# Sums of exponentials of an attention: folded on VectorE and summed by one small product, instead of a full product, a copy and a trip by DRAM

## The chip, the core and the metric

The kernel runs on one core of a Trainium2 chip. The metric is the device time of one execution in microseconds. Before the change it is 2647.13 us, the median of three runs (2646.86 to 2647.53). The profile is that of one execution, whose span is 2649.3 us. The engines are called TensorE (PE in the profile, its weight loads PEld), VectorE (DVE), ScalarE (ACT) and GpSimd (POOL); SyncE issues most of the loads.

## The reference, cut to what matters

Two graph layers over 16 graphs of 1024 nodes with 256 channels, all in float32. The first layer ends in an attention with four heads of 64 channels each:

```python
g = relu(einsum('bcn,bnm->bcm', fea, Wg) * para)      # queries, from the graph
kv = x @ kv_w                                          # keys and values
attn = softmax(einsum('bhnd,bhmd->bhnm', q, k) * scale, axis=-1)
out = einsum('bhnm,bhmd->bhnd', attn, v)
x = x + out
```

The second layer aggregates over the graph, then has two linear maps with batch normalisation. The change touches only the denominator of the softmax: for each query and each head the sum of the exponentials over 1024 keys.

## The kernel before, in words

**Units.** The attention is cut into 64 units: 16 graphs (b), 2 pairs of heads (k) and 2 halves of the queries (f, 512 each). A unit has two heads, numbered e. Scores are made transposed, keys on the partitions and queries along the columns. A unit is done in four steps (NG = 4), each over two blocks of 128 keys, so there are 256 steps and 16 of them to a graph.

**A step.** `attention()` writes the program step by step, and each engine runs its own instructions in that order; nothing reorders them later. In step s come: the scores of step s (`scores`, line 859 on TensorE, and the exponentials, line 867 on ScalarE); what is due at the top of the step; the additions of this step's exponentials into `acc` (lines 886 and 889 on VectorE); the values product of the step before (line 900); and then pieces of background work until a share of the graph's background is done. The background is everything else of the neighbouring graphs: keys and values, queries, the aggregation of the second layer, its first linear map, the norms. Its pieces have products on TensorE (line 159) and, behind them, evacuations and element-wise work on VectorE and ScalarE. A background piece may ask to be placed at the top of a step (`TOP`), as the transposes of line 384 do. `soon` puts an action behind the next piece.

**A unit's end.** When the values of a unit's last step are written, in step s = 4 x (number + 1), `acc` holds, for each of 128 partitions, two rows of 512 partial sums, one for each head. What is missing is the sum over the partitions. `sums()` makes it on TensorE at once: a product with 64 columns of ones for each head (line 917), so that every output row holds the sums. ScalarE copies the result into a tile `row` (line 919), GpSimd sends one row of each head to DRAM (line 920) and loads it back with the queries on the partitions (line 925). `finish()`, at the top of step s+2 (s+3 in graph 0, s+1 for the last two units), turns the unit's output with four transposes (line 935), and `add_output()` takes the reciprocal (line 943), multiplies (944), adds to x (950) and notes the extremes (952, 953).

**Buffers.** `ps_t` is one bank of PSUM, shared by the sums and the turned output. `row` is one of the four buffers of the tag `y`, which also serve the hidden layer's output (line 712), the columns of line 188, and `graph()`, which prepares combinations of the adjacency matrix on GpSimd during graph 0 and writes them to DRAM (lines 265 to 274). Background products alternate between two banks (`ps_mm`). GpSimd, like the others, runs its instructions in order, DMA issues among them.

Of the kernel before, what the change touches and what calls it, by code (L numbers as in the profile page):

```python
# [10 lines left out]
F32 = mybir.dt.float32  # L11
AF = mybir.ActivationFunctionType
ALU = mybir.AluOpType
AX = mybir.AxisListType
# [3 lines left out]
P = 128  # L18
# [5 lines left out]
def gnn_two_layers_kernel(  # L24
# [12 lines left out]
    nc = tc.nc  # L37
    B, N, C = x.shape
    H1 = w1_t.shape[1]
    NT = N // P  # L40
    CC = C // P
    HC = H1 // P
    HD = C // HEADS
    FB = 512
    NH = N // FB
# [6 lines left out]
    const = ctx.enter_context(tc.tile_pool(name="const", bufs=1))  # L52
    dram = ctx.enter_context(tc.tile_pool(name="dram", bufs=1, space=DRAM))

    ident = const.tile([P, P], F32, name="ident")
# [14 lines left out]
    y1_d = [dram.tile([P, HC, FB], F32, name=f"y1_d{i}") for i in range(B * NH)]  # L70

    dinv_d = dram.tile([N], F32, name="dinv_d")
    sums_d = [dram.tile([2, FB], F32, name=f"sums_d{u}") for u in range(B * CC * NH)]

    UNITS = B * CC * NH
    seen = const.tile([P, 2, UNITS], F32, name="seen")
    ones = const.tile([P, HD], F32, name="ones")
    nc.gpsimd.memset(ones, 1.0)

    def rsqrt(dst, src, add, tmp):  # L80

        nc.gpsimd.tensor_scalar_add(tmp, src, add)
        nc.gpsimd.tensor_tensor(dst, tmp, neg_half[:, : dst.shape[1]], op=ALU.pow)  # L83

    def layers(shifted):
# [9 lines left out]
        p1 = st.enter_context(tc.tile_pool(name=f"p1_{kind}", bufs=1))  # L95
        p2 = st.enter_context(tc.tile_pool(name=f"p2_{kind}", bufs=2))
        p3 = st.enter_context(tc.tile_pool(name=f"p3_{kind}", bufs=3))
        p8 = st.enter_context(tc.tile_pool(name=f"p8_{kind}", bufs=8))
        py = st.enter_context(tc.tile_pool(name=f"py_{kind}", bufs=4))
# [6 lines left out]
        ps_t = st.enter_context(tc.tile_pool(name=f"ps_t_{kind}", bufs=1, space=PSUM))  # L106
# [13 lines left out]
        def advance(pieces):  # L120

            due = queue[:]
            queue.clear()
            cost = next(pieces, None)
            for action in due:
                action()
            return cost

        def run(*parts):
            for part in parts:  # L130
                while advance(part) is not None:
                    pass
            while queue:
                queue.pop(0)()
# [75 lines left out]
        row, diag, col, deg, tmp_deg, dinv = (deg_sm[:, i, :] for i in range(6))  # L210
# [75 lines left out]
        class Norm:  # L286
# [3 lines left out]
            def __init__(self, b, first):  # L290
                tag = "a" if first else "b"
                self.src = xs[b]
                self.st6 = p2.tile([P, NT, 6], F32, tag="st6", name=f"st6_{tag}_{b}")
                self.mv = p2.tile([P, NT, 2], F32, tag="mv", name=f"mv_{tag}_{b}")
                self.sm = p2.tile([P, 3, NT], F32, tag="lnsm", name=f"lnsm_{tag}_{b}")
                self.csum = None
                if first:
                    self.csum = p2.tile([P, NT], F32, tag="csum", name=f"csum_{b}")
                    csums[b] = self.csum
                self.h = p2.tile([P, NT, C], F32, tag="h", name=f"h_{tag}_{b}")  # L300
                hs[tag, b] = self.h
# [569 lines left out]
        class Unit:  # L871
# [19 lines left out]
            def values(self, g, prs):  # L891
# [15 lines left out]
                if g == NG - 1:  # L907
                    self.os = p2.tile([P, FB], F32, tag="os", name=f"os_{self.name}")
                    nc.scalar.copy(self.os, self.o)

            def sums(self):

                u = self.index
                pt = ps_t.tile([P, FB], F32, tag="t", name=f"sums_{self.name}")
                for e in range(2):
                    r = slice(e * HD, (e + 1) * HD)
                    nc.tensor.matmul(pt[r, :], ones, self.acc[:, e, :], start=True, stop=True)
                row = py.tile([P, FB], F32, tag="y", name=f"row_{self.name}")
                nc.scalar.copy(row, pt)  # L919
                nc.gpsimd.dma_start(  # L920
                    out=sums_d[u], in_=row.rearrange("(e r) c -> e r c", r=HD)[:, 0, :]
                )
                self.inv = p2.tile([P, FB // P, 2], F32, tag="inv", name=f"inv_{self.name}")
                for e in range(2):
                    nc.gpsimd.dma_start(  # L925
                        out=self.inv[:, :, e], in_=sums_d[u][e].rearrange("(j q) -> q j", q=P)
                    )

            def finish(self):
# [10 lines left out]
            def add_output(self):  # L940
                b, k, f = self.at
                J, pt = FB // P, self.out
                nc.vector.reciprocal(self.inv, self.inv)
                nc.vector.tensor_mul(
                    self.os.rearrange("p (j e c) -> p j e c", j=J, e=2),
                    pt.rearrange("p (j e c) -> p j e c", j=J, e=2),
                    self.inv.unsqueeze(3).to_broadcast([P, J, 2, HD]),
                )
                dst = xs[b][:, f * J : (f + 1) * J, k * P : (k + 1) * P]
                nc.vector.tensor_add(dst, self.os.rearrange("p (j c) -> p j c", c=P), dst)  # L950
                inv = self.inv.rearrange("p j e -> p (j e)")
                nc.vector.tensor_reduce(seen[:, 0, self.index : self.index + 1], inv, AX.X, ALU.max)
                nc.vector.tensor_reduce(seen[:, 1, self.index : self.index + 1], inv, AX.X, ALU.min)
                if k == CC - 1:
                    complete.add((b, f))

        def attention():

            units = [Unit(b, k, f) for b in range(B) for k in range(CC) for f in range(NH)]
            steps = [(u, g) for u in units for g in range(NG)]  # L960
            per_graph = CC * NH * NG
            before = None
            pending = []
            bg, done, total, top = iter(()), 0.0, 0.0, False
            for s in range(len(steps) + 2):
                if s < len(steps):
                    unit, g = steps[s]
                    b = unit.at[0]
                    if s % per_graph == 0:
                        run(bg)  # L970
                        top = False
                        bg, done = background(b), 0.0
                        total = (37.6 if b > 0 else 41.0) * (b + 1 < B) + 24.0 * (b > 0) + 6.0 * (b + 2 < B)
                        total += 13.7 * (0 < b < B - 2) + 27.4 * (b == B - 1) + 3.0 * (b == 0)

                        total -= 10.3 * (b == B - 1)
                    made = scores(*unit.at, g)
                    due = total * (s % per_graph + 1) / per_graph
                else:
                    due += 5.1  # L980
                ended = None
                if pending and pending[0][1] <= s:
                    ended = pending.pop(0)[0]
                    ended.finish()
                if top:
                    done += advance(bg)
                    top = False
                if ended is not None:
                    ended.add_output()
                if s < len(steps):  # L990
                    for pr in made:
                        unit.add(pr)
                if before is not None:
                    (last, g_last), prs = before
                    last.values(g_last, prs)
                    if g_last == NG - 1:
                        last.sums()


                        later_by = 3 if last.at[0] == 0 else 2  # L1000
                        pending.append((last, s + (later_by if last.index < UNITS - 2 else 1)))
                while done < due and not top:
                    cost = advance(bg)
                    if cost is None:
                        break
                    if cost == TOP:
                        top = True
                        break
                    done += cost
                before = (steps[s], made) if s < len(steps) else None  # L1010
            run(bg)

        with st:
# [22 lines left out]
            else:  # L1036
# [20 lines left out]
                load_x(2)  # L1057
                run(weave(plain_queries(0), (0, weighers[0]), (5, Norm(1, True).all())))
                attention()
                attn.close()  # L1060
                turns.append(second(kind))
# [267 lines left out]
    ext = fp.tile([P, 4], F32, name="ext")  # L1329
# [8 lines left out]

    def flag(good):

        nc.tensor.matmul(good[0:1, :], ext[:, 2:3], ones[:, 0:1], start=True, stop=True)
        nc.vector.tensor_scalar(bad, good[0:1, :], -1.0, float(P), op0=ALU.mult, op1=ALU.add)

    with tc.manual_schedule():
        layers(False)

    again = nc.values_load(bad[0:1, 0:1], min_val=0, max_val=P)  # L1347
    with tc.If(again > 0):
        layers(True)
# [37 lines left out]
```

## Time and profile before

| | busy us | share of 2649.3 us |
|---|---|---|
| TensorE | 2571.1 | 97% |
| VectorE | 1741.8 | 66% |
| ScalarE | 1335.5 | 50% |
| GpSimd | 561.2 | 21% |

| lines of the sums | engine | count | mean ns |
|---|---|---|---|
| 917 product with ones | TensorE | 256 passes | 592, overlapping |
| 919 copy to `row` | ScalarE | 64 | 586 |
| 920 row to DRAM | GpSimd | 64 | 586 to issue, 1.7 us to land |
| 925 back from DRAM | GpSimd | 128 | 771 to issue, 2.7 us to land |
| 943 reciprocal | VectorE | 64 | 193 |
| 935 transposes of the output | TensorE | 256 | 286, overlapping |

A busy time adds up what an engine's instructions last. TensorE's matmuls overlap one another, so the cost of one is read from the distance between starts, not from its length. A line of the profile's timeline has the start, the length, the engine, the line of the kernel, the operation, the tiles (output <- inputs), shapes and count; in brackets stands how long the engine was idle before it and what released it. A float32 product appears as two passes, and a product of two 64-column halves as four. The clock row shows the share of TensorE's full clock that was granted. Attention begins with the scores of step 0 at 61.7 us and ends near 2324 us; then come the rest of the last graph's aggregation and the second linear map.

### The profile page before, as it was taken

The page shows a single profiled execution, that of the slowest core. Times are in us where ns is not written, and L with a number is a line of the kernel's source. Part 1 is how long each engine was busy: PE and PEld are TensorE (multiplying, and loading weights), DVE is VectorE, ACT ScalarE, POOL GpSimd, SP SyncE. Part 2 cuts the span into 40 slices and gives each one's busy share as a digit, 9 for nine tenths or more (in the row PEclk, how much of TensorE's full clock was granted, in tenths as well). Part 3 has the DMA queues.
Part 4 walks back from the last instruction along what each step waited for, and adds up shares of the span by engine and source line. Part 5 has one row for each costly group of instructions (what it writes and reads, how often), then busy time and mean ns, then how long its engine had stood idle before and what let it go on. Part 6 is the DMA issues. An engine that isn't in the chain of part 4 may idle for free. (4 is left out here: it accounts for less than half of the span.)

```text
span 2649.3 us, 32166 instructions
## 1 busy us (share of the span) xinstructions
PE 2571.1 (97%) x11874; PEld 951.7 (36%) x11874; DVE 1741.8 (66%) x2766; ACT 1335.5 (50%) x1935; POOL 561.2 (21%) x648
## 2 busy tenths in 40 slices
PE   8979999999999999999999999999999999999994
PEld 3333333333333333333333333333333333334443
DVE  5648576766667675757666676757576675557675
ACT  5745454636364554546363645545463634335544
POOL 1451111021111111110211111111111112026653
PEclk9989999999999999999999999999999999999997
DMA  4453414242423323152525242332424232355559
GB/s 159 149 177 109 146 61 171 84 171 80 166 78 135 100 96 136 60 175 80 172 80 175 68 144 92 103 133 65 166 80 171 80 132 96 134 196 204 193 179 377
DMA packets 132870, 356.12 MB, mean 134 GB/s; under 512 B 19040, under 2 KB 35936, under 8 KB 126560
## 3 DMA queue, kind: packets, MB, share of 16 engines
q1 hardware_dynamic: 105952, 274.77, 29.7%
q0 software_dynamic: 26752, 79.20, 8.9%
q8 instruction: 96, 1.57, 0.2%
q14 instruction: 70, 0.57, 0.1%
HBM read 279.19 MB, written 74.72 MB: 134 GB/s over the span
## 5 line engine op out<-in xcount | busy, mean ns | idle before, releaser
L867 ACT ACTIVATE p<-sc 128x1024 f32<-128x1024 f32 x512 | 495.4, 1020 | 610.3 <-PE sc L859 609.8
L889 DVE TENSOR_TENSOR acc<-acc,p 128x1024 f32<-128x1024 f32 x384 | 470.9, 1226 | 135.5 <-ACT p L867 115.1
L859 PE MATMUL sc<-q,k 64*128 64x512 f32 x2048 | 510.2, 617 | 14.2 <-ACT p L867 14.2
L900 PE MATMUL o<-p,v 128*64 128x512 f32 x2048 | 497.6, 607 | 0.0
L159 PE MATMUL pg<-w,h_a 128*64 128x512 f32 x1600 | 358.1, 592 | 3.4 <-ACT k L600 1.7
L159 PE MATMUL pa<-aht,h_b 128*64 128x512 f32 x1536 | 343.7, 592 | 0.0
L859 PEld LDWEIGHTS sc<-q,k 64*128 64x128 f32 x2048 | 176.6, 186 | 335.0 <-issue 298.0
L920 POOL DMA_DIRECT2D sums_d<-row x64 | 37.5, 586 | 1031.8 <-ACT row L919 1031.8
L159 PE MATMUL py<-at,w 128*64 128x512 f32 x1024 | 230.4, 592 | 0.0
L900 PEld LDWEIGHTS o<-p,v 128*64 128x64 f32 x2048 | 124.6, 136 | 286.0 <-issue 284.5
L413 DVE SCALAR_TENSOR_TENSOR w<-w,adj 128x1024 f32<-128x1024 f32 x128 | 158.0, 1235 | 101.7 <-ACT w L434 97.8
L159 PEld LDWEIGHTS pg<-w,h_a 128*64 128x64 f32 x1600 | 115.5, 137 | 231.8 <-issue 213.1
L159 PEld LDWEIGHTS pa<-aht,h_b 128*64 128x64 f32 x1536 | 111.2, 137 | 212.6 <-issue 196.6
L713 ACT ACTIVATE y<-py,vec 128x512 f32<-128x512 f32 x128 | 87.6, 684 | 167.9 <-PE py L159 111.4
L426 ACT ACTIVATE w<-cbc,csum 128x512 f32<-128x512 f32 x256 | 170.0, 715 | 0.0
L886 DVE TENSOR_TENSOR acc<-p,p 128x1024 f32<-128x1024 f32 x64 | 78.9, 1233 | 109.3 <-ACT p L867 109.3
L714 POOL DMA_DIRECT2D y_d<-y x128 | 70.1, 547 | 316.1 <-ACT y L713 315.5
L434 ACT ACTIVATE w<-w 128x1024 f32<-128x1024 f32 x128 | 134.9, 1054 | 1.8
L488 DVE TENSOR_TENSOR w<-w,w 128x1024 f32<-128x1024 f32 x112 | 132.7, 1215 | 1.5
L925 POOL DMA_DIRECT2D inv<-sums_d x128 | 98.2, 771 | 138.7 <-DMA sums_d<-row 102.2
L159 PEld LDWEIGHTS py<-at,w 128*64 128x64 f32 x1024 | 74.3, 137 | 145.1 <-issue 128.2
L717 DVE BATCH_NORM_STATS2 stats<-y 128x6 f32<-128x512 f32 x128 | 85.4, 686 | 59.3 <-ACT y L713 57.4
(151 smaller groups left out, 2892.9 us busy)
## 6 DMA issues: line engine op xcount, KB each, us to landing
aht<-aht_d SPq DMA_DIRECT2D x224, 512.0 KB, 6.4
adj<-in_adj_dram SPq DMA_DIRECT2D x128, 512.0 KB, 4.4
y_d<-y POOLq DMA_DIRECT2D x128, 256.0 KB, 2.6
yin_f<-y_d SPq DMA_DIRECT2D x32, 1024.0 KB, 6.3
x<-in_x_dram SPq DMA_DIRECT2D x32, 512.0 KB, 5.0
para<-in_para_dram SPq DMA_DIRECT2D x64, 256.0 KB, 3.8
x_d<-x POOLq DMA_DIRECT2D x16, 1024.0 KB, 10.5
xo_f<-x_d SPq DMA_DIRECT2D x32, 512.0 KB, 8.7
```

The lines of the kernel that those rows point to most:

```text
L159: nc.tensor.matmul(dst[r], left[:, r], right, start=start, stop=stop)
L413: nc.vector.scalar_tensor_tensor(w, w, 1.0, a, op0=ALU.add, op1=ALU.mult)
L426: nc.scalar.activation(w[:, t, :], cbc[:, q * FB : (q + 1) * FB], AF.Abs, bias=csum[:, th * TH + t : th * TH + t + 1], scale=-1.0,)
L434: nc.scalar.activation(made[i], made[i], AF.Tanh, scale=-0.5 / C)
L488: nc.vector.tensor_sub(block(i)[part], block(x)[part], block(y)[part])
L713: nc.scalar.activation(y, made, AF.Identity, bias=b1[:, j : j + 1])
L717: nc.vector.bn_stats(stats1[:, j, i, :], y)
L859: nc.tensor.matmul(sc[:, e, :], ks[b][k][r, m * P : (m + 1) * P], qs[b][k][r, f * FB : (f + 1) * FB], start=True, stop=True,)
L867: nc.scalar.activation(pr, sc, AF.Exp)
L889: nc.vector.tensor_add(self.acc, self.acc, pr)
L900: nc.tensor.matmul(self.o[r, :], vs[b][k][:, m, r], pr[:, e, :], start=(m == 0), stop=(m == NT - 1),)
L925: nc.gpsimd.dma_start(out=self.inv[:, :, e], in_=sums_d[u][e].rearrange("(j q) -> q j", q=P))
```

## The change

The sums are made in another way, with no copy by ScalarE and no trip by DRAM. At a unit's end VectorE turns `acc` of one head in squares of 32x32 into PSUM and sums each run of 32 elements (`fold`). After that, partition 32a + r holds, in column c, the sum of query 32c + r over the 32 keys of group a. What is still to be added are the four groups a. A product with the constant table `same` (ones where the row and the column have the same remainder by 32) does this for both heads at once, with only 32 columns; its output has the queries on the partitions already, and four reciprocals, one for each quarter of the partitions, put them in place in `inv`.

The steps are laid out anew: the fold of head 0 comes at the end of step s, behind that step's background, that of head 1 at the end of step s+1; the product and the reciprocals at the top of step s+2; the transposes and the addition at the top of step s+3. The last unit does all of it in s and s+1. `st6` and `mv` of the norms go from two buffers to one, and `ones` to one column.

```diff
-    sums_d = [dram.tile([2, FB], F32, name=f"sums_d{u}") for u in range(B * CC * NH)]
...
+    SQ = 32
+    NS = P // SQ
+    same = const.tile([P, NS, SQ], F32, name="same")
+    nc.vector.tensor_reduce(
+        same[:, 0, :], ident.rearrange("p (a r) -> p r a", r=SQ), AX.X, ALU.add
+    )
+    for i in range(1, NS):
+        nc.vector.tensor_copy(same[:, i, :], same[:, 0, :])
...
-                self.st6 = p2.tile([P, NT, 6], F32, tag="st6", name=f"st6_{tag}_{b}")
-                self.mv = p2.tile([P, NT, 2], F32, tag="mv", name=f"mv_{tag}_{b}")
+                self.st6 = p1.tile([P, NT, 6], F32, tag="st6", name=f"st6_{tag}_{b}")
+                self.mv = p1.tile([P, NT, 2], F32, tag="mv", name=f"mv_{tag}_{b}")
...
+            def fold(self, e):
+                if e == 0:
+                    self.part = p1.tile([P, 2, FB // SQ], F32, tag="part", name=f"part_{self.name}")
+                pt = ps_t.tile([P, FB], F32, tag="t", name=f"turned_{self.name}_{e}")
+                nc.vector.transpose(pt, self.acc[:, e, :])
+                nc.vector.tensor_reduce(
+                    self.part[:, e, :], pt.rearrange("p (c s) -> p c s", s=SQ), AX.X, ALU.add
+                )
+
             def sums(self):
-                pt = ps_t.tile([P, FB], F32, tag="t", name=f"sums_{self.name}")
-                for e in range(2):
-                    r = slice(e * HD, (e + 1) * HD)
-                    nc.tensor.matmul(pt[r, :], ones, self.acc[:, e, :], start=True, stop=True)
-                row = py.tile([P, FB], F32, tag="y", name=f"row_{self.name}")
-                nc.scalar.copy(row, pt)
-                nc.gpsimd.dma_start(
-                    out=sums_d[u], in_=row.rearrange("(e r) c -> e r c", r=HD)[:, 0, :]
-                )
+                pt = ps_t.tile([P, FB], F32, tag="t", name=f"sums_{self.name}")[:, : 2 * FB // SQ]
+                nc.tensor.matmul(
+                    pt,
+                    same.rearrange("p a r -> p (a r)"),
+                    self.part.rearrange("p e c -> p (e c)"),
+                    start=True,
+                    stop=True,
+                )
                 self.inv = p2.tile([P, FB // P, 2], F32, tag="inv", name=f"inv_{self.name}")
-                for e in range(2):
-                    nc.gpsimd.dma_start(
-                        out=self.inv[:, :, e], in_=sums_d[u][e].rearrange("(j q) -> q j", q=P)
+                for a in range(NS):
+                    r = slice(a * SQ, (a + 1) * SQ)
+                    nc.vector.reciprocal(
+                        self.inv[r].rearrange("p j e -> p e j"),
+                        pt[r].rearrange("p (e j a) -> p a e j", e=2, a=NS)[:, a],
                     )
...
-                nc.vector.reciprocal(self.inv, self.inv)
...
+                for action in at_top.pop(s, ()):
+                    action()
                 if top:
                     done += advance(bg)
                     top = False
-                if ended is not None:
-                    ended.add_output()
+                if s in adds:
+                    adds.pop(s)()
...
                     if g_last == NG - 1:
-                        last.sums()
-                        later_by = 3 if last.at[0] == 0 else 2
-                        pending.append((last, s + (later_by if last.index < UNITS - 2 else 1)))
+                        n = 0 if last.index == UNITS - 1 else 1
+                        for e in range(2):
+                            at_end.setdefault(s + n * e, []).append(lambda u=last, e=e: u.fold(e))
+                        at_top.setdefault(s + 1 + n, []).append(last.sums)
+                        at_top.setdefault(s + 1 + 2 * n, []).append(last.finish)
+                        adds[s + 1 + 2 * n] = last.add_output
...
+                for action in at_end.pop(s, ()):
+                    action()
```

More of the change, by code (lines that the diff above doesn't have):

```diff
@@ L72, in gnn_two_layers_kernel @@
     dinv_d = dram.tile([N], F32, name="dinv_d")
-    sums_d = [dram.tile([2, FB], F32, name=f"sums_d{u}") for u in range(B * CC * NH)]
     UNITS = B * CC * NH
     seen = const.tile([P, 2, UNITS], F32, name="seen")
-    ones = const.tile([P, HD], F32, name="ones")
+    ones = const.tile([P, 1], F32, name="ones")
     nc.gpsimd.memset(ones, 1.0)
+    SQ = 32
[6 more added lines that the diff above has]
+        nc.vector.tensor_copy(same[:, i, :], same[:, 0, :])
     def rsqrt(dst, src, add, tmp):
@@ L909, in values @@
                     nc.scalar.copy(self.os, self.o)
-            def sums(self):
-                u = self.index
-                pt = ps_t.tile([P, FB], F32, tag="t", name=f"sums_{self.name}")
-                for e in range(2):
-                    r = slice(e * HD, (e + 1) * HD)
-                    nc.tensor.matmul(pt[r, :], ones, self.acc[:, e, :], start=True, stop=True)
-                row = py.tile([P, FB], F32, tag="y", name=f"row_{self.name}")
-                nc.scalar.copy(row, pt)
-                nc.gpsimd.dma_start(
-                    out=sums_d[u], in_=row.rearrange("(e r) c -> e r c", r=HD)[:, 0, :]
+            def fold(self, e):
[6 more added lines that the diff above has]
+                )
+            def sums(self):
+                pt = ps_t.tile([P, FB], F32, tag="t", name=f"sums_{self.name}")[:, : 2 * FB // SQ]
[5 more added lines that the diff above has]
+                    stop=True,
                 )
                 self.inv = p2.tile([P, FB // P, 2], F32, tag="inv", name=f"inv_{self.name}")
-                for e in range(2):
-                    nc.gpsimd.dma_start(
-                        out=self.inv[:, :, e], in_=sums_d[u][e].rearrange("(j q) -> q j", q=P)
+                for a in range(NS):
[3 more added lines that the diff above has]
+                        pt[r].rearrange("p (e j a) -> p a e j", e=2, a=NS)[:, a],
                     )
@@ L962, in attention @@
             before = None
-            pending = []
+            at_top, at_end, adds = {}, {}, {}
             bg, done, total, top = iter(()), 0.0, 0.0, False
@@ L980, in attention @@
                     due += 5.1
[L981 to L984, printed above, removed]
+                for action in at_top.pop(s, ()):
+                    action()
                 if top:
@@ L1339, in flag @@
     def flag(good):
-        nc.tensor.matmul(good[0:1, :], ext[:, 2:3], ones[:, 0:1], start=True, stop=True)
+        nc.tensor.matmul(good[0:1, :], ext[:, 2:3], ones, start=True, stop=True)
         nc.vector.tensor_scalar(bad, good[0:1, :], -1.0, float(P), op0=ALU.mult, op1=ALU.add)
```

## The prediction, made before the changed kernel was run

> **What bounds the kernel now.** I read the engine totals first, then what TensorE waits for, then the stretch in which one unit of attention ends, then the place in VectorE's queue where the change puts its work.
>
> ```profile
> PE 2571.1 (97%) x11874; PEld 951.7 (36%) x11874; DVE 1741.8 (66%) x2766; ACT 1335.5 (50%) x1935; POOL 561.2 (21%) x648
> ```
> ```profile
> PE sc L859 <- ACT p L867: 14.2, 2, 13.7
> PE htp L384 <- ACT h_a L329: 8.2, 1, 8.2
> ```
> TensorE is busy 97% of the span, and the longest sum of waits of any of its lines is 14.2 us, nearly all one wait of 13.7 us. In the attention stage, then, a TensorE instruction removed shortens the run, and a wait put into TensorE's queue lengthens it by all of its length: there is almost no slack to take it from.
>
> ```profile
> 1215.66 1.94 PE L900 MATMUL o<-p,v 128*64 128x512 f32 x8
> 1217.42 1.03 PE L917 MATMUL sums<-acc,ones 128*64 128x512 f32 x4
> 1218.28 0.60 PE L159 MATMUL pk<-ht,kvw_f 128*64 128x512 f32 x2
> ```
> This is the timeline at a unit's end. The sums' product stands from 1217.42 to the next start at 1218.28: **0.86 us** of TensorE (the matmul's printed time overlaps the next one).
>
> ```profile
> 1269.65 1.99 PE L859 MATMUL sc<-q,k 64*128 64x512 f32 x8
> 1271.57 0.66 PE L935 MATMUL ot<-ident,os 128*128 128x128 f32 x4
> 1271.31 0.69 DVE L522 TENSOR_TENSOR q<-pg,q 128x512 f32<-128x512 f32 x1
> 1272.33 0.16 DVE L315 TENSOR_TENSOR lnsm_b<-lnsm_b,deg 128x4 f32<-128x4 f32 x1 [0.33 <-POOL lnsm_b L83]
> 1272.52 0.16 DVE L318 SCALAR_TENSOR_TENSOR lnsm_b<-mv_b,lnsm_b 128x4 f32<-128x4 f32 x1
> 1272.61 0.20 DVE L943 RECIPROCAL inv<-inv 128x8 f32<-128x8 f32 x1
> ```
> Two engines at one place of the program: the top of the second step after a unit's last. TensorE gets there at 1271.57, when its scores are issued (today it starts the ot transposes). VectorE has by then not finished the background of the step before: L318 ends at 1272.68, and only then comes L943, the first instruction of the top. VectorE is 1.11 us behind. Nobody minds today, since TensorE waits for nothing of VectorE here.
>
> ```profile
> 154.76 0.59 ACT L909 COPY os<-o 128x512 f32<-128x512 f32 x1 [0.73 <-PE o L900]
> 174.97 0.59 ACT L919 COPY row<-sums 128x512 f32<-128x512 f32 x1 [19.63 <-DMA aht_d<-two]
> 131.98 0.57 POOL L920 DMA_DIRECT2D sums_d<-row  x1
> 139.47 1.55 POOL L925 DMA_DIRECT2D inv<-sums_d  x2 [6.92 <-DMA sums_d<-row]
> ```
> The one long wait comes from the old way of the sums. In graph 0 the copy into row needs one of the four y buffers; they hold what graph() writes out, so ScalarE stands 19.63 us, and the exponentials behind it. The writes are late because GpSimd itself stood from 131.98 to 141.02 (9.0 us) on the trip by DRAM.
>
> ```profile
> 163.00:176.50 13.50, 0.00 (x0) 0.00 (x0) 0.76 (x1) 1.53 (x3) 13.19 (x20) 0.60 0.60 212
> 176.50:180.00 3.50, 3.46 (x9) 1.31 (x10) 0.00 (x0) 1.92 (x2) 3.34 (x6) 0.58 0.51 172
> 184.00:188.00 4.00, 4.00 (x13) 1.21 (x13) 3.69 (x4) 3.41 (x6) 0.52 (x1) 0.50 0.13 1
> 1213.00:1358.00 145.00, 144.81 (x696) 51.75 (x694) 97.99 (x157) 74.12 (x109) 22.43 (x29) 1.00 0.34 117
> ```
> Windows: length, busy PE, PEld, DVE, ACT, POOL, granted clock, DMA. The stop drops the clock to about half until some 190 us. An inner graph lasts 145 us, TensorE busy 144.8, VectorE 98: VectorE has room on the average, so what counts is where its work is put.
>
> **What the Trainium skill says.** TensorE: Matmul & The Clock Gate, Step-by-step: only weight loads are pulled ahead, matmuls stay in program order; this trace agrees, as no product passes a waiting one at 176.5. So a waiting sums product holds everything behind it. PSUM — Partial Sum Buffer, Engine vs sequencer instructions: VectorE's queue is strictly first in, first out; the trace agrees (L943 above sits behind L315's wait). The clock gate page, Part 1, names windows of about 3.4 us after which an idle array is slowed; the trace agrees in kind (clock 0.58 and 0.50 above). As a price: VectorE: DVE Perf Modes, The three transpose paths, gives 311 ns for 128x128 in 32x32 blocks, in bf16 and into SBUF; no run here shows that operation.
>
> **The change, part by part.**
>
> *TensorE.* Gone: 64 x 0.86 = 55.0 us. New: one product with 128x128 weights and 32 columns. In f32 a product is two passes; four passes of 128x128 weights and 128 columns (ot) take 0.66 us, so two take at most about 0.33, and the two passes of the one-column product L1341 take 0.16. I take 0.30, 64 x 0.30 = 19.2. Net gain **36 us**.
>
> *VectorE's fold.* A turn of 128x512 into PSUM and a sum over 32s. Price of the turn: from below 0.53 us (512 elements at one per 0.96 GHz cycle by the page's clock, no fixed cost), from above double the copy L387 (128x512 out of PSUM, 0.686 us), 1.37, if 4-byte elements go at half rate. From the page's 311 ns for 128 and this trace's slope for reduces, (1209 - 286) / 896 = 1.03 ns an element (L416, L223), I take 0.70. Sum: 286 + 384 x 1.03 = 0.68 us. With two gaps of 0.03, a fold is **1.44 us**; ends 1.2 and 2.1. Two per unit are 184 us of VectorE; four reciprocals at L943's 0.19 instead of one add 37. Off the path, on the average: 14 us more in a graph of 145 us with 47 idle.
>
> *The wait.* The second fold is queued at the end of step s+1, behind that step's background; the sums product follows the scores of step s+2 and reads it. So TensorE waits (VectorE's lag at this place) + 1.44 + 0.1 for handing over. The lag, end of the background minus start of ot (or htp), in the four units of an inner graph: 1234.42 - 1234.39 = 0.03 (behind L413); 1.11 (above); 1308.98 - 1309.21 = -0.23 (behind L307); 1344.68 - 1343.98 = 0.70 (behind L717). Sum 1.61. In the second unit the first fold, too, pushes: it falls into a stretch where VectorE is dense, with 1.0 us of gaps to swallow 1.44, so 0.4 more. Per graph 1.61 + 0.4 + 4 x 1.54 = **8.2 us**, and the same rows repeat in graphs 1 to 13: 107 us. Behind the waiting product stand the values of step s+1 and the background products; ScalarE then waits for TensorE. In the last two graphs VectorE is less loaded: by the same reading 0 to 3.8 us a unit, 14 in all, and 3 for the last unit, where no scores lie between and the transposes wait for the reciprocals too: 17. Graph 0: 4.
>
> *ScalarE and GpSimd.* 64 copies of 0.586 and 192 DMA issues go: 37 and 136 us, all off the path except in graph 0. There ScalarE needs no y buffer, and GpSimd's graph() runs at least 9 us ahead, so the column copies that use y next on VectorE hardly wait. Gained: 13.7, the 2.9 us wait after it, and half of the 9 us at half clock: **21 us**.
>
> *Later finish.* The output is added at s+3 instead of s+2 (s+3 in graph 0 already). Inner graphs start the next norm later than that anyway; for the last graph I put 3 us into the 17. Single buffers for st6 and mv: nothing, since a norm's readers are through before the next norm begins. The table same: under 1 us before x has arrived.
>
> *Clock.* Waits of 3 us come near the 3.4 us windows; if a quarter of the 13 drop it and cost about 3 us each: 10 us.
>
> Sum: 107 + 17 + 4 - 36 - 21 + 10 = +81, so 2647 + 81 = **2728 us**.
>
> **Rivals.**
> (a) *The folds are hidden*, VectorE reaching them 1.5 us earlier than I read: only the gains stay, 2647 - 36 - 21 = 2590. For it: VectorE's 66%. Against: the lag rows above, where even the best unit has only 0.23 us in hand. Chance 0.10.
> (b) *Half the waits*: a fold nearer 1.2 us and some lag gone, since TensorE itself now arrives later after each wait: 2647 - 57 + 64 = 2654, and from there to 2680. For it: VectorE catches up during a wait. Against: the lags arise within the step before, from TensorE's own products. 0.08: 0.05 of it slower, 0.02 no change, 0.01 faster.
> (c) *Turn at half rate, or clock drops at each long wait*: a fold of 2.0 adds 0.56 x 62 = 35 us, drops add 30 more: 2765 to 2800. For it: a 4-byte turn and PSUM as its target are unseen. 0.12.
>
> **How the numbers follow.** The forecast has 0.70; 2680 to 2775 holds it, the dear end of (b) and the cheap end of (c). Slower: 0.70 + 0.12 + 0.05 = 0.87; within 0.2%: 0.02; faster: 0.10 + 0.01 = 0.11.
>
> **What would show it.** Right: TensorE's waits list the sums product behind VectorE's reduce, some 62 times, about 2 us each and 110 to 140 us in all, the second unit of a graph the worst at 3; a turn and a reduce of 0.7 us each; VectorE near 1960 us busy; no 13.7 us wait in graph 0, and TensorE's busy share near 93%. Wrong: if a fold takes 1.2 us or less, or if VectorE stands ready before TensorE arrives; or if other TensorE products come to wait for VectorE's later evacuations, which I put at nothing because two banks leave each of them a product's time.

## The result, and the profile after

The changed kernel takes **2754.49 us**, the median of four runs (2751.68 to 2757.04); the kernel before took 2647.33 (2646.86 to 2648.39) beside it. The ratio is **1.0405 [1.039, 1.0421]**: 107 us slower, where 81 were forecast. The profiled run of the changed kernel has a span of 2755.1 us, against 2649.3. The profiled execution of the kernel before took 2651.18 us, 4 us more than its median, so that differences between profiles and between medians differ by some microseconds. The lines of the kernel have moved: scores are L867, values L908, the turn L925, the reduce L926, the sums product L933, the reciprocals L943, the output's transposes L954, background products L167.

First the engine totals of the changed kernel.

```profile
PE 2572.7 (93%) x11746; PEld 963.4 (35%) x11746; DVE 1957.3 (71%) x3218; ACT 1298.8 (47%) x1871; POOL 394.1 (14%) x456
```

TensorE has 128 instructions less, but not less busy time: 64 x 0.86 us were meant to leave. Part of its work now ran at a lower clock, as shown below; in e3, an experiment below with the same TensorE instructions and no such drops in the inner graphs, it is busy 2537.5 us. Its share fell from 97% to 93%: 182 us of the span are idle (2755.1 - 2572.7), against 78 before (2649.3 - 2571.1).

Next, from the waits of the changed kernel, the longest one of TensorE.

```profile
PE sums L933 <- DVE part L926: 121.8, 60, 6.3
```

Microseconds in all, times, the longest: 60 of the 64 sums products wait for VectorE's reduce, 121.8 us together. The second on TensorE's list is the wait for ScalarE's `h_a` before attention begins, 8.4 us, which was 8.2 before; the wait of 13.7 us in graph 0 is gone. Now the groups of the changed kernel that make up the new way (busy, mean ns of one, then the idle time just before).

```profile
L933 PE MATMUL sums<-part,same 128*128 128x32 f32 x128 | 27.3, 297 | 121.8 <-DVE part L926 121.8
L925 DVE STREAM_TRANSPOSE turned<-acc 128x512 f32<-128x512 f32 x128 | 91.1, 712 | 0.0
L926 DVE TENSOR_REDUCE part<-turned 128x16 f32<-128x512 f32 x128 | 88.5, 692 | 4.4
```

The turn and the reduce cost 0.71 and 0.69 us, and VectorE idles almost nowhere ahead of them: a fold starts as soon as its turn in the queue comes. That is the clue that the fold waits behind other work, not for data.

The timeline of the changed kernel at the end of the second unit of graph 1 shows one such wait.

```profile
241.89 1.99 PE L867 MATMUL sc<-q,k 64*128 64x512 f32 x8
246.98 0.41 PE L933 MATMUL sums<-part,same 128*128 128x32 f32 x2 [3.10 <-DVE part L926]
247.32 1.94 PE L908 MATMUL o<-p,v 128*64 128x512 f32 x8
...
245.40 0.16 DVE L326 SCALAR_TENSOR_TENSOR lnsm_b<-mv_b,lnsm_b 128x4 f32<-128x4 f32 x1
245.48 0.72 DVE L925 STREAM_TRANSPOSE turned<-acc 128x512 f32<-128x512 f32 x1
246.24 0.69 DVE L926 TENSOR_REDUCE part<-turned 128x16 f32<-128x512 f32 x1
```

TensorE's scores end at 243.9, and the sums product is next in its queue. VectorE gets through the background of the step before at 245.5 (L326, as foreseen), then folds until 246.93, and 0.05 later the product starts. TensorE has stood for 3.10 us. ("Second" counts the places of a graph's stretch at which a unit ends. The first place belongs to the last unit of the graph before, so the second is that of the graph's own first unit.) The other units of an inner graph wait 1.09, 1.99 and 1.38 us by the same reading; together **7.56 us** a graph. From the product's start to that of the values (246.98 to 247.32) it costs 0.34 us.

Some waits cost more than their length. Four windows of the changed kernel, two places in graph 2: length, busy PE, PEld, DVE, ACT, POOL, granted clock, DMA share, GB/s.

```profile
394.00:399.00 5.00, 1.90 (x10) 0.78 (x10) 4.03 (x12) 4.81 (x8) 2.16 (x3) 1.00 0.71 210
399.20:402.40 3.20, 3.20 (x16) 1.65 (x14) 2.04 (x2) 0.01 (x1) 0.00 (x0) 0.50 0.91 326
470.80:474.10 3.30, 1.31 (x11) 0.77 (x8) 2.75 (x6) 2.41 (x3) 0.20 (x1) 1.00 0.70 233
474.30:477.50 3.20, 3.20 (x10) 1.02 (x10) 3.05 (x6) 0.00 (x0) 0.00 (x0) 0.50 0.02 5
```

The first and the third hold a wait of the sums product of 3.10 and of 1.99 us. In the two that follow, TensorE is busy all the time at half clock. Such a drop lasts 3.41 us and so costs about half of it, 1.7.

The wait of 3.10 us in graph 1 was followed by no drop. The 19 drops of the inner graphs begin within 0.001 us of one grid of 3.4133 us (at 399.095, 474.188, 552.695 and so on). Three cells of this grid, two across the wait in graph 1 and the one ahead of the first drop of graph 2:

```profile
242.08:245.50 3.42, 1.79 (x8) 0.49 (x6) 3.06 (x11) 2.89 (x5) 2.23 (x3) 1.00 0.22 56
245.50:248.91 3.41, 1.93 (x10) 0.93 (x12) 2.81 (x8) 3.23 (x6) 0.27 (x1) 1.00 0.92 264
395.68:399.10 3.42, 1.64 (x8) 0.78 (x10) 2.78 (x9) 3.42 (x6) 0.56 (x1) 1.00 0.95 276
```

The grid cuts the wait of graph 1 in two: TensorE is idle for 1.63 and 1.48 us of the two cells. In graph 2 1.78 us of idle time fall into one cell, and half clock follows in the next. Over graphs 1 to 13, the cell ahead of each of the 19 drops has 1.78 to 2.79 us of idle time, and none of the other 562 cells has more than 1.83. So whether a wait costs clock depends on its length and on where the grid cuts it. This is read from the trace; no run moved a wait against the grid.

Where the 105.8 us between the two profiled runs come from, by the starts of the scores from graph to graph:

| stretch | before | after | difference |
|---|---|---|---|
| start of attention | 61.7 | | -0.6 |
| graph 0 | 135.1 | 124.6 | -10.5 |
| graph 1, no drop of the clock | 145.2 | 150.6 | +5.4 |
| graphs 8 and 9, no drop | 145.2 | 150.5 | +5.2 each |
| graph 7, one drop | 145.4 | 152.2 | +6.8 |
| graphs 2 to 6 and 10 to 13, two drops each | 145.2 | 153.8 | +8.6 each |
| graphs 14 and 15 | 230.2 | 237.3 | +7.1 |
| after the last scores | | | +10.2 |

An inner graph without a drop checks the account: waits 7.56, where before only `pv` waited 0.19; old products away 4 x 0.86 = 3.44, new ones 3 x 0.34 + 0.24 = 1.26 (the one ahead of the htp transposes costs 0.24). So 7.56 - 0.19 - 3.44 + 1.26 = 5.19, and 5.2 to 5.4 were measured. The two drops account for the rest: 153.81 - 150.48 = 3.33 = 2 x 1.67. Graphs 1 to 13 give 99.7 us in all, 19 x 1.67 = 32 of it by the clock.

### The profile page after: what moved, and what is told of

Read it like the earlier page. It is cut to its first block, busy times and chain, and to the rows that moved or that the text cites. A ratio compares the mean times of both kernels' runs of the same rounds, so it can differ in the third digit from the quotient of the medians.

```text
span 2755.1 us, 31827 instructions
## 1 busy us (share of the span) xinstructions
PE 2572.7 (93%) x11746; PEld 963.4 (35%) x11746; DVE 1957.3 (71%) x3218; ACT 1298.8 (47%) x1871; POOL 394.1 (14%) x456
## 4 chain that ended last, share of the span: by engine, by line
PE 75%; DVE 13%; DMA 3%; POOL 3%; ACT 3%; issue 2%; SPq 0%; POOLq 0%; DVEq 0%; ACTq 0%
PE o L908 16%; PE pa L167 14%; PE sc L867 12%; PE pg L167 8%; PE m_f L1202 7%; PE py L167 6%; PE pv L167 4%; PE pk L167 4%; DVE w L421 2%; DMA out_dram<-xo_f 2%; DVE part L926 2%; DVE turned L925 2%; PE ot L954 1%; DVE st_b L313 1%; DVE acc L897 1%
## 5 line engine op out<-in xcount | busy, mean ns | idle before, releaser
L908 PE MATMUL o<-p,v 128*64 128x512 f32 x2048 | 517.0, 627 | 0.0
L867 PE MATMUL sc<-q,k 64*128 64x512 f32 x2048 | 508.8, 615 | 0.5 <-ACT p L875 0.5
L167 PE MATMUL pg<-w,h_a 128*64 128x512 f32 x1600 | 358.1, 592 | 3.6 <-DVE q L588 1.9
L167 PE MATMUL pa<-aht,h_b 128*64 128x512 f32 x1536 | 344.1, 592 | 0.7 <-ACT h_b L337 0.6
L867 PEld LDWEIGHTS sc<-q,k 64*128 64x128 f32 x2048 | 176.1, 186 | 320.6 <-issue 295.4
L167 PE MATMUL py<-at,w 128*64 128x512 f32 x1024 | 231.7, 595 | 0.0
L908 PEld LDWEIGHTS o<-p,v 128*64 128x64 f32 x2048 | 127.9, 140 | 259.8 <-issue 257.7
L167 PEld LDWEIGHTS pg<-w,h_a 128*64 128x64 f32 x1600 | 115.5, 137 | 232.0 <-issue 210.5
L167 PEld LDWEIGHTS pa<-aht,h_b 128*64 128x64 f32 x1536 | 111.1, 137 | 214.6 <-issue 205.9
L933 PE MATMUL sums<-part,same 128*128 128x32 f32 x128 | 27.3, 297 | 121.8 <-DVE part L926 121.8
L442 ACT ACTIVATE w<-w 128x1024 f32<-128x1024 f32 x128 | 135.1, 1056 | 1.8
L167 PEld LDWEIGHTS py<-at,w 128*64 128x64 f32 x1024 | 74.2, 138 | 147.4 <-issue 139.3
L90 POOL TENSOR_SCALAR lnsm_b<-mv_b 128x4 f32<-128x4 f32 x32 | 12.2, 380 | 791.9 <-DVE mv_b L315 791.8
L167 PE MATMUL pv<-kvw_f,ht 128*64 128x256 f32 x1024 | 123.7, 396 | 0.4 <-DVE v L625 0.4
```

The lines of the kernel that those rows point to most:

```text
L167: nc.tensor.matmul(dst[r], left[:, r], right, start=start, stop=stop)
L442: nc.scalar.activation(made[i], made[i], AF.Tanh, scale=-0.5 / C)
L867: nc.tensor.matmul(sc[:, e, :], ks[b][k][r, m * P : (m + 1) * P], qs[b][k][r, f * FB : (f + 1) * FB], start=True, stop=True,)
L908: nc.tensor.matmul(self.o[r, :], vs[b][k][:, m, r], pr[:, e, :], start=(m == 0), stop=(m == NT - 1),)
```

## The experiments

**Two theories.** The *queue theory* is that of the prediction: TensorE waits because the fold is queued behind the background, and its consumer stands at the top of the next step; the same fold at another place, or the same product a little later, costs nothing. Its rival, the *load theory*, holds that VectorE has no room for 184 us of folds where the attention is dense: put elsewhere, they delay other work that TensorE waits for, so that the wait only changes its name. All kernels but the last two start from the changed kernel; only e4 does work that is of no use. The first four were run beside one another (before: 2646.61 us), as were the last four (before: 2648.39).

**The second fold ahead of the background.** In step s+1 the fold of head 1 comes right after the values instead of after the background.

```diff
-                            at_end.setdefault(s + n * e, []).append(lambda u=last, e=e: u.fold(e))
+                            where = mid if n * e else at_end
+                            where.setdefault(s + n * e, []).append(lambda u=last, e=e: u.fold(e))
...
+                for action in mid.pop(s, ()):
+                    action()
                 while done < due and not top:
```

> The changed kernel with one move: the second fold of a unit stands in front of the background of step s+1 instead of behind it; everything else, VectorE's work included, is as in the changed kernel. Queue theory (the loss is TensorE waiting at the sums product for a fold that is queued behind a background): the product finds its input ready, the 122 us of waits fall under 15 us, and with them nearly all clock drops after attention's start (20 of 3.4 us at half clock, 34 us); 2754 - 122 - 32 = 2600, at most 2620 us. Load theory (VectorE's 215 us of new work are too much for the stage wherever they stand): the waits come back at other products, which wait for evacuations that the fold now delays; TensorE's busy share stays near 93% and the time above 2700 us.

2633.61 us; ratio to before 0.9951 [0.9934, 0.9967]. The same instructions in another order are 121 us faster than the change. TensorE's two longest waits in this kernel:

```profile
PE pv L167 <- DVE v L625: 21.9, 14, 1.7
PE sums L933 <- DVE part L926: 9.9, 3, 5.2
```

In the inner graphs the sums product waits no more, and no drop of the clock is left there; its three waits are in graph 0 (0.70 and 5.24 us) and at the last unit (4.01). But a product of the background, `pv`, now waits once a graph, 1.65 us, for VectorE's copy of `v`, which the fold pushed back (it waited 0.19 before). An inner graph takes 144.51 us, 0.73 less than before; without any wait it would be 2.37 less (3.44 - 1.26 + 0.19), and 2.37 - 1.65 = 0.72. So the queue theory has the large part, and the load theory a small true one, which is why the time missed the expected range.

**The product a little later, folds as they were.** The sums and the reciprocals move from the top of step s+2 to behind its values product.

```diff
-                        at_top.setdefault(s + 1 + n, []).append(last.sums)
+                        (mid if n else at_top).setdefault(s + 1 + n, []).append(last.sums)
...
+                for action in mid.pop(s, ()):
+                    action()
```

> The changed kernel with one move: the sums product and its reciprocals stand behind the values product of step s+2 instead of in front of it; the folds stay where they are. Queue theory: TensorE arrives 1.76 us later, so each wait shrinks by 1.76 us and no further: 3.17 to 1.4, 2.05 to 0.3, 1.15 and 1.44 to 0, in all some 36 us of waits instead of 122, and few clock drops: 2754 - 86 - 29 = 2639 us, 2625 to 2655. Load theory: above 2700 us.

2643.17 us, 0.9991 [0.9983, 1.0], inside the expected range. Between the scores and the product there are now 1.9 us of TensorE work, and each wait is shorter by about that: the second unit of an inner graph waits 1.24 us instead of 3.10, the others nothing. In all L933 waits 28.0 us, 17 times, where it was 121.8. An inner graph is at 144.98; from the waits (1.24, and 0.10 of `pv`) and the products, 3.44 - 4 x 0.34 + 0.19 - 1.34 = 0.93 less than before would follow, and 0.26 was measured. The other 0.67 is at the new place itself: in graph 8 the values products take 28.75 us from start to start, waits left out, instead of 28.28, and the background products behind the four sums products 0.2 more. Why was not tried.

**The product a whole step later.** The sums at the top of s+3, the transposes and the addition at s+4; the folds stay behind the background.

```diff
-                        at_top.setdefault(s + 1 + n, []).append(last.sums)
-                        at_top.setdefault(s + 1 + 2 * n, []).append(last.finish)
-                        adds[s + 1 + 2 * n] = last.add_output
+                        at_top.setdefault(s + 1 + 2 * n, []).append(last.sums)
+                        at_top.setdefault(s + 1 + 3 * n, []).append(last.finish)
+                        adds[s + 1 + 3 * n] = last.add_output
```

> The changed kernel with the sums product and reciprocals at the top of step s+3 and the transposes and the addition at the top of step s+4 (the last unit as before); the folds stay where they are. Queue theory: no wait at the sums product save the last unit's, 2754 - 118 - 33 = 2603 us, 2590 to 2620. Load theory: above 2700 us. If the later addition holds the norms up, waits appear at the aggregation's products of the last graph.

2626.73 us, 0.9924 [0.9908, 0.9941]: the sums product waits nowhere in the inner graphs, and the drops went with its waits. The timeline of this kernel around the same second unit of graph 1:

```profile
236.07 0.72 DVE L925 STREAM_TRANSPOSE turned<-acc 128x512 f32<-128x512 f32 x1
236.82 0.69 DVE L926 TENSOR_REDUCE part<-turned 128x16 f32<-128x512 f32 x1
239.90 0.75 DVE L625 COPY v<-pv 128x256 f32<-128x256 f32 x2
...
240.79 1.95 PE L167 MATMUL pv<-kvw_f,ht 128*64 128x256 f32 x16 [1.65 <-DVE v L625]
...
244.59 0.41 PE L933 MATMUL sums<-part,same 128*128 128x32 f32 x2
```

The product at 244.59 has no bracket: it found its input there. What is left is the wait of `pv` for the copies of `v`, 14.4 us over the run. In most inner graphs it is 1.00 us, and 3.44 - 1.26 + 0.19 - 1.00 = 1.37 comes near the 1.23 us that such a graph gained. The time missed the expected range by 7 us: the waits of `pv` were not expected. Against the kernel before, 12.3 us are lost after the last scores, where the last unit's folds are still behind the background; its product waits 5.1 us and its transposes 1.0. One wait fits the last expected sign: in the stretch of the last graph a product of the aggregation (`pa`) waits 2.7 us for ScalarE's `h_b`. It waited there neither before the change nor in the changed kernel.

**The fold made longer.** The reduce done twice.

```diff
                 nc.vector.tensor_reduce(
                     self.part[:, e, :], pt.rearrange("p (c s) -> p c s", s=SQ), AX.X, ALU.add
                 )
+                nc.vector.tensor_reduce(
+                    self.part[:, e, :], pt.rearrange("p (c s) -> p c s", s=SQ), AX.X, ALU.add
+                )
```

> The changed kernel with each fold's reduce done twice into the same place (the second has no use): 0.69 us more per fold, 88 us more of VectorE. Queue theory: each of some 56 waits grows by 0.69 us, and in the second unit of 13 graphs by 0.69 more for the first fold's push: +48 us, and more clock drops, up to +25: 2800 to 2830 us. If the waits were hidden behind something else that bounds the stage: within 10 us of 2754.

2822.3 us, 1.0665 [1.0647, 1.0683], inside the expected range. The wait of the sums product in this kernel:

```profile
PE sums L936 <- DVE part L929: 175.2, 62, 7.8
```

121.8 became 175.2, 53 us for 62 waits. In an inner graph three units wait 0.72 us longer, which is the one further reduce, and the second unit 1.44 longer, as there the first fold pushes the second. At these places every microsecond of a fold is one of TensorE. The rest of the 68 us by which the time rose, some 15, goes with a lower mean clock (0.971 of full speed was granted, 0.977 in the changed kernel).

**Toward a better version: the last unit's folds ahead.** e3, with both folds of the last unit in front of the background of its last step.

```diff
-                            at_end.setdefault(s + n * e, []).append(lambda u=last, e=e: u.fold(e))
+                            where = at_end if n else mid
+                            where.setdefault(s + n * e, []).append(lambda u=last, e=e: u.fold(e))
...
+                for action in mid.pop(s, ()):
+                    action()
```

> The version of run e3 (sums at the top of step s+3) with one more move: the last unit's two folds stand in front of the background of its last step instead of behind it. Queue theory: the last unit's product (wait 5.1 us, then 1.0 us at the transposes, then a clock drop of 6.8 us at half speed) waits for nothing, 5.1 + 1 + 3.4 = 9.5 us less: 2627 - 9.5 = 2617 us, 2613 to 2622. If the end is set by the last norm and not by this wait: within 3 us of 2627.

2620.05 us, 0.9893 [0.9878, 0.9908], inside the expected range. The wait of 5.1 us at the last sums product is gone; the transposes behind it still wait 2.8 us for the reciprocals. Against the kernel before, the median is lower by 28.3 us and the profiled span by 31.6: 19.4 in graph 0, 15.6 in graphs 1 to 13, 1.1 at the start, 1.5 in the last two graphs, and 6.0 given back after the last scores.

**The second unit's fold later still.** e5, with the second fold of each graph's dense unit a step later, so that the copies of `v` come ahead of it.

```diff
-                            where.setdefault(s + n * e, []).append(lambda u=last, e=e: u.fold(e))
+                            at = s + n * e * (2 if last.index % 4 == 0 else 1)
+                            where.setdefault(at, []).append(lambda u=last, e=e: u.fold(e))
```

> The version of run e5 with the second fold of every graph's first unit one step later, at the end of step s+2, behind the value copies that TensorE waits for in run e3 (14 waits of 1.03 us). Those waits go (-14 us); the fold then ends some 0.6 us behind TensorE's arrival at the top of step s+3 (the lag there is -0.96 us before the change, plus 1.54), 14 x 0.6 = +8: 6 us less than e5, between 2605 and 2614. If the value copies are late for another reason: no less than e5.

2619.07 us, 0.9893 [0.9878, 0.9908]. The once-a-graph wait for `v` went, the sums product waits 0.29 us in its place, and an inner graph takes 143.42 us, 0.59 less than in e5: 7.7 us over 13 of them. Of this, 1.8 was lost again before attention began and 2.6 in graph 14, where a sums product waits 2.55 us. By the medians, 1 us apart, e5 and e6 can't be told apart, and the expected range was missed.

**What graph 0 was worth.** Two kernels put the block of graph 0 to the test in the kernel *before*. In the first, the old way of the sums stays, but in graph 0 the copied row goes into `acc`, which is free by then, and the trip by DRAM is issued by SyncE.

```diff
+                first = self.at[0] == 0
+                dma = nc.sync if first else nc.gpsimd
-                row = py.tile([P, FB], F32, tag="y", name=f"row_{self.name}")
+                if first:
+                    row = self.acc[:, 0, :]
+                else:
+                    row = py.tile([P, FB], F32, tag="y", name=f"row_{self.name}")
...
-                nc.gpsimd.dma_start(
+                dma.dma_start(
...
-                    nc.gpsimd.dma_start(
+                    dma.dma_start(
```

> The kernel before the change; in graph 0 alone the row of sums lies in acc instead of a y buffer, and the trip by DRAM is issued by SyncE instead of GpSimd. If the gain in graph 0 comes from ScalarE no longer standing for a y buffer and GpSimd no longer standing for the trip: the 13.7 us wait goes with its clock drop, 17 to 21 us less than before: 2626 to 2630 us. If it comes from the fold itself: no change. The loads that SyncE holds up behind the trip could take some of it back.

2632.93 us, 0.9943 [0.9929, 0.9956]. Graph 0 takes 113.79 us instead of 135.13, 21.3 us less, which is the 21 that the prediction put on this block. The median gained 15.5 of it and came out 3 us above the expected range. Of the other 5.9, 4.8 come from which executions were profiled: the one of the kernel before has a span of 2649.3, the median one beside this run 2646.6, and the profiled one of this run, 2629.1, lies 2.1 below its own median one. The last 1.1 was given back outside graph 0. So what graph 0 gains in a median execution is known only to some microseconds.

> The kernel before the change; in graph 0 alone the row of sums lies in acc instead of a y buffer; the trip stays with GpSimd. ScalarE no longer stands for the buffer, but GpSimd still stands 9 us, so what graph() writes lands as late as before and VectorE's column copies stand in ScalarE's place: 0 to 6 us less than before, 2641 to 2647 us. If the buffer alone was the cause: 2627 us.

2642.74 us, 0.9979 [0.9972, 0.9986], inside the expected range. In this second kernel, with the row out of `y`, but the trip still on GpSimd, graph 0 gains 7.6 us only. The block comes back elsewhere. VectorE's column copy in this kernel:

```profile
173.31 1.33 DVE L189 COPY cb_c<-csum 128x512 f32<-128x512 f32 x2 [16.20 <-POOL two L265]
```

It stands 16.20 us for `graph()` on GpSimd, and TensorE's transposes of these columns wait 10.1 us in their turn. So the shared buffer alone was 7.6 us of the block, and the other 13.7 hung on GpSimd's in-order trip as well.

## Why the prediction was right

The mechanism held: the reduce bounds TensorE at each unit's end, at the places and with nearly the sizes that were read from VectorE's lag. Rival (a), folds hidden, failed, as 60 of 64 products waited. Rival (b), half the waits, failed too: 7.56 us a graph, not half of 8.2. Rival (c) had two parts; the half-rate turn did not come (0.712 us), while the drops of its other part did, 32 us, though on the forecast's fold and not on a longer one.

By the terms of the sum:

- *The fold*, 1.44: 1.45 measured (245.48 to 246.93). The turn was a guess between 0.53 and 1.37; the reading off a bf16 price and this kernel's own slope gave 0.70, and 0.712 was measured. That a price for bf16 into SBUF carries over to float32 into PSUM rested on no run, so its nearness is in part luck.
- *Inner waits*, 107: 13 x 7.56 = 98. The second unit came out at 3.10 for 3.05; the others waited 0.2 us less than read, 1.99 for 2.24 in the unit with a lag of 0.70.
- *Net gain of TensorE*, 36: 64 x 0.86 less 64 products of 0.34 (more than the "at most about 0.33") or 0.24, so 34 to 35.
- *Graph 0*, -21 and +4: -10.5 came. e7 shows a block worth 21.3 in the profiles, so the other term was too small: the sums products there waited some 10 us instead of 4, and one stretch of 6.8 us at half clock came on top. The timeline of the changed kernel shows the longest of them, and what stands a few microseconds ahead of it on VectorE:

```profile
165.15 1.25 DVE L197 COPY cb_c<-csum 128x512 f32<-128x512 f32 x2 [5.10 <-POOL au_f L277]
...
172.29 0.63 PE L933 MATMUL sums<-part,same 128*128 128x32 f32 x2 [5.62 <-DVE part L926]
```

  "The column copies hardly wait" was wrong: they stood 5.10 us for GpSimd, and from 165.15 on VectorE works without a gap (copies of `v`, a fold, additions, the second fold) until the reduce ends at 172.24, when the product starts. So the 5.10 us arrive at TensorE through the queue. GpSimd was itself later than in e7: the last of its operations `two<-au_f` (L273 here, L265 there) starts at 162.57 us, against 157.15. Some of these operations last 1.7 us instead of 0.7, in both kernels; why was not tried.
- *Last graphs and the end*, 17 in waits: 9.5 in the stretch of the last two graphs and 5.0 at the last unit (4.0 for the reduce and 1.0 for the reciprocals), 14.5. But the clock fell there too, for 6.8 us at the last unit and 3.4 soon after, and the stretch after the last scores lost 10.2 in all.
- *Clock*, 10: this is **the term that was mis-sized**. It was a quarter of 13 waits at 3 us each. In fact 19 drops fell in the inner graphs, 32 us. Each cost 1.67 us and not 3, but they came after the waits of 2.0 us as well as after those of 3.1, in 10 of 13 graphs. By stretches, with TensorE's gain of 2.25 us a graph counted in each, graph 0 is 8.7 us above the sum, the inner graphs 12 (22 more by the clock, 10 less by waits and products), graph 14 to the end 4.8, and the start 0.6 below. Together these are the 25 us by which the span's growth, 105.8, exceeds the 81 of the sum.
- *Evacuations at nothing*: true of the changed kernel, where L167's waits for L625 are 0.4 us. It hid a limit, however: once the sums no longer held TensorE back, in e1 and e3, the copies of `v` were late by 1.0 to 1.65 us a graph.
- *Later finish, single buffers*: e3 moves the finish a further step back, and no wait for the output shows in the inner graphs, only the 2.7 us in the last one. The single buffers were not tried by themselves; in the changed kernel no wait of TensorE's names them, which leaves a small cost by another path open.

The forecast's direction thus came from one row of the timeline before: VectorE still at its background while TensorE asks. What the change saves is real, 1.1% in e5; of that about half is the block in graph 0 (15.5 of 28.3 us by the medians), which e7 removes from the kernel before without any new way of the sums.

## What to carry to other kernels

A cheaper product is not cheaper if its input comes from another engine's in-order queue and the consumer stands where that queue runs late: read the lag of the producing engine at that very place, then add the new work to it. Put the producer ahead of the background or the consumer one step later; here the same instructions took 2754 us in one order and 2620 in the other. A wait of 2 to 3 us on a busy TensorE is to be priced with the clock drop that may follow (1.7 us here), and an old detour is to be checked for what else it holds back, for that may be the better half of the gain.

## What the runs showed of the hardware

- **Waits of 2.0 us can cost clock, by where they fall.** The Trainium skill (TensorE: Matmul & The Clock Gate, Why this matters for your kernels) says to keep TensorE's gaps under about 3 us. Here less was enough: in the inner graphs waits of 1.99 us were followed by 3.41 us at half clock in nine graphs, while waits of 1.09 and 1.38 us never were. The page's Part 1 speaks of a window that runs free of the program, and the trace agrees: the drops of the inner graphs lie on a grid of 3.4133 us, and each follows a cell with 1.78 us or more of idle time. In graphs 1, 8 and 9, where no drop came, the grid cut the waits of 3.1 and 1.99 us so that no cell had more than 1.74. With drops a graph lasts 153.81 us, 45.06 cells, so the place of a wait in its cell repeats from graph to graph with a slow drift.
- The turn of 128x512 float32 in 32x32 squares takes 712 ns into PSUM, the reduce of 128x512 from PSUM in runs of 32 takes 692 ns.
- A float32 product with 128x128 weights and 32 columns costs TensorE 0.34 us from its start to that of the values product, and 0.24 to that of small transposes. Two of the transposes with 128 columns take 0.29 in the kernel before (four from 1234.39 to 1234.97), so a quarter of the columns was not a quarter of the time.
- A reciprocal of 32 partitions x 8 takes 204 ns (L943 after) and one of 128 x 8 takes 193 (L943 before): here a quarter of the partitions took no less time.
